# Node sums one column group ahead of the update, and a narrower last pair of tiles, in a two-layer graph network

## The chip, the core and the metric

The kernel runs on one core of a Trainium2 chip. The metric is device time in microseconds. Before the change it is 3391.78 us, the median of nine runs (3369.91 to 3401.86).

## The reference

3125 nodes with 256 features and 100,000 edges, sorted by destination, go through two layers. In each layer the features are normalised, a graph network and an attention over all nodes are added to them, and then a routed feed-forward network (mixture of experts) is added. Cut to what matters here:

```python
# layer 0, graph part: twice
agg = segment_sum(x[col], row)               # sums over neighbours
h = (x + agg / max(deg, 1)) @ W.T + b
x = silu((h - mean) * rsqrt(var + eps) * g + beta)
# layer 0, experts: 8 experts, 256 -> 1024 -> 256, the best two of each node
# layer 1, graph part: attention over the edges; then linear attention; then
# layer 1, experts: 6 experts, 256 -> 256 -> 256 -> 256, the best two of each node
h1 = relu(x @ w1[e] + b1[e]); h2 = relu(h1 @ w2[e] + b2[e]); y = h2 @ w3[e] + b3[e]
out = x + sum over the two best experts of weight * y
```

## The kernel before

**Layout.** Nodes lie in 25 tiles of 128 rows (`NB` = 25); the last tile has `LAST` = 53 real rows. `xs` holds the running features of all tiles in SBUF.

**Layer 0's graph part** (in `fast`, from line 2790). The kernel has made a dense count matrix `adj` (3125 by 3200, bf16, in DRAM) out of the edges, so that neighbour sums are matrix products. The two graph layers are one loop `for layer in range(2)`; inside it one loop goes over column groups of destination nodes: `GROUPS` is six groups of 512 columns and one of 128, and `GROUPS1`, used in the second graph layer, is five of 512, two of 256 and one of 128. They are numbered 0 to 6 and 0 to 7 below. For one column group at column `c` of width `cw`:

- *Sums.* Two PSUM tiles `agg0`, `agg1` (two slots each) collect 25 source tiles. For each source tile a bf16 piece `at` (loaded by SP, 640 KB for five source tiles, four slots) is cast to `wide` (five slots), on ScalarE (line 2834) or VectorE (line 2836) by turns, and four matmuls (line 2839) multiply it with the tile's features `px`, kept as a high and a low part. So a group has 100 matmuls. In the second graph layer the group at column 0 also makes `px` anew (`two_parts`, lines 2276 to 2278) from `yn`, which the first graph layer has written. In the first graph layer SP also issues the clearing of the experts' input table here.
- *Update.* VectorE makes `zt` from `agg`, the degrees and `xt` (lines 2844, 2845; two slots). For each 128 columns TensorE multiplies with the layer's weights (`hp`, line 2853, one slot), VectorE adds the bias and takes the statistics; then comes the normalisation and ScalarE's silu. In the first graph layer the result goes to `yn` and, transposed, back to `xt`. In the second it is added to `xs`, and `T_.tokens` routes the nodes: normalisation twice, transposes (line 375), router matmuls `lg` (line 2360), softmax and top two, positions in the experts' table (`slot`), and two scatters by POOL for each tile (line 2413) of the routed rows `x2`. `x2` has the tag `zt`, so both share its two slots; most of the small tiles of `tokens` have one slot. `tokens` of the groups depend on each other through the running count `base`.

After the last group come `T_.plan` and `T_.results`, which turn the counts into a plan, and then the experts of layer 0 (`experts`; first a transpose, line 2613).

**What sets the order there.** This part is not written out by hand: the framework's planner orders each engine's instructions when the program is built. It goes through an estimated run, and for an engine that is free it takes, among the instructions whose inputs and slots are there, the one that stands first in the program. Afterwards each engine runs its list strictly in that order. The experts of layer 0, and all of layer 1's graph part and experts, have a hand-written order instead (`manual_schedule`).

**Layer 1's experts** (`Layer1.group`). Node tiles are taken together in groups of two or three (`TOGETHER`); the last is tiles 23 and 24. For each of six experts there are two hidden layers, each of two halves `j`: two matmuls with the weights as the stationary side and the group's features as the moving side, `W = nt * 128` columns (line 1494; each f32 matmul is two records in the trace), then a relu on ScalarE (line 1497); `hp` has two slots. Then `result` multiplies the hidden features with the third weights (line 1563) and VectorE adds them, weighted, to `xs` (line 1569). Groups are spread as filler over the blocks of edges by `take`; the last group is queued when the last block's nodes are done, so it runs alone at the end of the kernel.

Of the kernel before, what the change touches and what calls it, by code (L numbers as in the profile page):

```python
# [11 lines left out]
AF = mybir.ActivationFunctionType  # L12
# [6 lines left out]
P = 128  # L19
NB = 25  # L20
NP = NB * P
LAST = N - (NB - 1) * P
GROUPS = [(c, min(512, NP - c)) for c in range(0, NP, 512)]
# [5 lines left out]
W = 8  # L29
# [942 lines left out]
GROUPS1 = GROUPS[:5] + [(2560, 256), (2816, 256), (3072, 128)]  # L972
# [379 lines left out]
class Layer1:  # L1352
# [121 lines left out]
    def group(self, t0, nt, xt):  # L1474
        nc, wk, ps, xs = self.nc, self.wk, self.ps, self.xs
        W, u = nt * P, nt / 4
        sh = [P, nt, NE1]
        k = lambda name, *d: wk.tile([P, GB] + list(d), F32, name=name, bufs=1)[:, :nt]
        bc = lambda x: x[:, :, None].to_broadcast(sh)
        ws = {}  # L1480
# [10 lines left out]
        def layer(i, e, x, o, j):  # L1491
            hp = ps.tile([P, 512], F32, name="hp", bufs=2)
            for n in range(2):
                nc.tensor.matmul(hp[:, :W], ws[i, e][:, n, j * P:(j + 1) * P], x[:, n, :W], start=(n == 0),  # L1494
                                 stop=(n == 1))
            b = self.bc1 if i == 1 else self.bc2
            nc.scalar.activation(o[:, j, :W], hp[:, :W], AF.Relu, bias=b[:, e, j:j + 1])  # L1497

        h1, h2 = {}, {}
        hid = lambda name: wk.tile([P, 2, GB * P], F32, name=name)  # L1500
# [48 lines left out]
        wgt = wk.tile([P, GB, NE1], F32, name="wgt")[:, :nt]  # L1549
# [9 lines left out]
        def result(e, i0):  # L1559
            y = two()  # L1560
            for i in range(i0, min(i0 + 2, nt)):
                for n in range(2):
                    nc.tensor.matmul(y[:, i - i0, :], h2[e][:, n, i * P:(i + 1) * P], ws[3, e][:, n, :],  # L1563
                                     start=(n == 0), stop=(n == 1))

            def add():
                for i in range(i0, min(i0 + 2, nt)):
                    t = t0 + i
                    nc.vector.scalar_tensor_tensor(xs[:, t, :], y[:, i - i0, :], wgt[:, i, e:e + 1], xs[:, t, :],  # L1569
                                                   op0=OP.mult, op1=OP.add)  # L1570
                    if e == NE1 - 1:
                        n = P if t < NB - 1 else LAST
                        self.stores.append((self.out[t * P:t * P + n, :], xs[:n, t, :]))
            self.late.append(add)

# [1111 lines left out]
def fast(ctx: ExitStack, tc: tile.TileContext, a, out, flag):  # L2687
    nc = tc.nc
# [102 lines left out]
    with tc.tile_pool(name="g", bufs=1) as g1, tc.tile_pool(name="ga", bufs=4) as ga, \  # L2791
            tc.tile_pool(name="gt", bufs=2) as gt, \
            tc.tile_pool(name="gg", bufs=2, space=PSUM) as gg, \
            tc.tile_pool(name="gp", bufs=1, space=PSUM) as gp:
        wr = load_k(nc, g1, a["L0_ffn_Wr"], "wr", nc.scalar)
        br = g1.tile([P, NE0], F32, name="br")
        nc.scalar.dma_start(br, row_bc(a["L0_ffn_br"], NE0))
        once = gt.tile([P, D], F32, name="z")[:SH, :P]
        nc.vector.tensor_reduce(once, deg[:SH].rearrange("p (k l) -> p l k", l=P), AX.X, OP.add)
        nc.vector.tensor_scalar(once, once, 1.0, None, op0=OP.max)  # L2800
        nc.vector.reciprocal(once, once)
        nc.sync.dma_start(degrees, once)
        clear = T_.clear(tc, zero)
        for t in range(0, NB, 2):
            mix.result(t, mix_p, gt, gam, xs)
        yn = nodes.tile([P, NB, D], F32, name="yn", tag="late")
        for layer in range(2):
            w = load_k(nc, g1, a[f"L0_gnn_W{layer}T"], f"gw{layer}")
            rows = {}
            for name in ("b", "g", "beta"):  # L2810
                rows[name] = g1.tile([P, D], F32, name=f"row_{name}", tag=f"row_{name}{layer}")
                nc.scalar.dma_start(rows[name], row_bc(a[f"L0_gnn_{name}{layer}"], D))
            for c, cw in (GROUPS if layer == 0 else GROUPS1):
                agg = [gg.tile([P, 512], F32, name=f"agg{g}") for g in range(2)]
                rdeg = gt.tile([P, 512], F32, name="rdeg")[:, :cw]
                nc.scalar.dma_start(rdeg, degrees.rearrange("s l -> (s l)")[None, c:c + cw].to_broadcast([P, cw]))
                for kb in range(NB // KB):
                    at = ga.tile([P, KB, 512], BF, name="at")
                    k0 = kb * KB
                    m = KB if k0 + KB < NB else KB - 1  # L2820
                    nc.sync.dma_start(at[:, :m, :cw], adj[k0 * P:(k0 + m) * P, c:c + cw].rearrange(
                        "(k p) s -> p k s", p=P))
                    if m < KB:
                        nc.sync.dma_start(at[:LAST, m, :cw], adj[full:N, c:c + cw])
                    for _ in range(4 if layer == 0 and c else 0):
                        next(clear, None)
                    for i in range(KB):
                        k = k0 + i
                        n = P if k < NB - 1 else LAST
                        if layer == 1 and c == 0:  # L2830
                            two_parts(nc, gt, px[:, 0, k, :], px[:, 1, k, :], yn[:, k, :], [P, D])
                        wide = ga.tile([P, 512], F32R, name="wide", bufs=5)
                        if (i + layer) % 2:
                            nc.scalar.copy(wide[:n, :cw], at[:n, i, :cw])  # L2834
                        else:
                            nc.vector.tensor_copy(wide[:n, :cw], at[:n, i, :cw])
                        for g in range(2):
                            for j in range(2):
                                nc.tensor.matmul(agg[g][:, :cw], px[:n, j, k, g * P:(g + 1) * P],  # L2839
                                                 wide[:n, :cw], start=(k == 0 and j == 0),  # L2840
                                                 stop=(k == NB - 1 and j == 1))
                zt = gt.tile([P, 2, 512], F32, name="zt")
                for g in range(2):
                    nc.vector.tensor_tensor(zt[:, g, :cw], agg[g][:, :cw], rdeg, OP.mult)
                    nc.vector.tensor_add(zt[:, g, :cw], zt[:, g, :cw], xt[:, g, c:c + cw])
                nt = cw // P
                h = gt.tile([P, 4, D], F32, name="h")
                st = gt.tile([P, 4, 6], F32, name="st")
                mv = gt.tile([P, 4, 2], F32, name="mv")
                for i in range(nt):  # L2850
                    hp = gp.tile([P, D], F32, name="hp")
                    for k in range(2):
                        nc.tensor.matmul(hp, zt[:, k, i * P:(i + 1) * P], w[:, k, :], start=(k == 0),
                                         stop=(k == 1))
                    nc.vector.tensor_add(h[:, i, :], hp, rows["b"])
                    nc.vector.bn_stats(st[:, i, :], h[:, i, :])
                    nc.vector.bn_aggr(mv[:, i, :], st[:, i, :])
                rs = gt.tile([P, 4], F32, name="rs")
                nc.vector.tensor_scalar(rs[:, :nt], mv[:, :nt, 1], EPS, None, op0=OP.add)
                nc.scalar.activation(rs[:, :nt], rs[:, :nt], AF.Sqrt)  # L2860
                nc.vector.reciprocal(rs[:, :nt], rs[:, :nt])
                for i in range(nt):
                    t = c // P + i
                    z = gt.tile([P, D], F32, name="z")
                    nc.vector.scalar_tensor_tensor(z, h[:, i, :], mv[:, i, 0:1], rows["g"],
                                                   op0=OP.subtract, op1=OP.mult)
                    nc.vector.scalar_tensor_tensor(z, z, rs[:, i:i + 1], rows["beta"], op0=OP.mult, op1=OP.add)
                    y = yn[:, t, :] if layer == 0 else gt.tile([P, D], F32, name="y")
                    nc.scalar.activation(y, z, AF.Silu)
                    if layer == 0:  # L2870
                        transposed(nc, C, gp, xt[:, :, t * P:(t + 1) * P], y)
                    else:
                        nc.vector.tensor_add(xs[:, t, :], xs[:, t, :], y)
                if layer == 1:
                    T_.tokens(tc, C, gt, gp, xs, c // P, nt, wr, br)
        T_.plan(nc, C, gt)
    big.close()
    late = ctx.enter_context(tc.tile_pool(name="late", bufs=1))
# [196 lines left out]
```

## Time and profile before

| | |
|---|---|
| median of nine runs | 3391.78 us (3369.91 to 3401.86) |
| profiled execution, its own time | 3373.52 us |
| its span, first to last instruction | 3371.5 us |
| mean granted TensorE clock | 0.816 |
| first graph layer's first sums | start at 371.5 us |
| second graph layer's last sums | end at 818.5 us |
| layer 0's experts, first transpose | 852.3 us |
| last pair of layer 1's experts | 3321.0 to 3364.6 us |

The profile is of one execution. "Granted clock" is the TensorE clock as a share of full speed. In a timeline row the first number is the start in us, the second the duration, then engine, line, operation, output from input, and how many instructions were merged; in brackets stands how long the engine was idle before it and what released it. A matmul's end is modelled, so consecutive matmul rows overlap a little; starts are the better measure. A row whose letters are cut, such as `x` for `x2`, names the tile without its number.

### The profile page before, as it was taken

The numbers are of one execution on the slowest core, as the hardware profiler recorded it, in microseconds if no ns is written. First come the engines' busy times: TensorE is split into PE (matmuls) and PEld (weight loads), VectorE is DVE, ScalarE is ACT, GpSimd is POOL, SyncE is SP. The second block draws the span as 40 slices with busy tenths as digits, with TensorE's granted clock in tenths as the row PEclk, the third lists the DMA queues.
The fourth block names the chain that finished last, engine by engine and source line by source line (L and its number), as shares of the span: only waits on it lengthen the run. The fifth ranks groups of instructions, "written<-read, shape, count | busy, mean of one in ns | idle before, by whom it ended". The sixth has DMA issues, their size and how long they took to land.

```text
span 3371.5 us, 35817 instructions
## 1 busy us (share of the span) xinstructions
PE 2338.2 (69%) x11721; PEld 1608.7 (48%) x11721; DVE 1690.2 (50%) x4297; ACT 902.4 (27%) x1982; POOL 1040.4 (31%) x1101
## 2 busy tenths in 40 slices
PE   4899899997777998897254536355465756545678
PEld 2555677776556887343232323243233323333446
DVE  8988766686200222632153546365546545444463
ACT  3444234553112222221121110122122212212223
POOL 1000000122463000502434444535546455454310
PEclk9999999995878999898566656687677868776789
DMA  4333596433445666545332334344435434443432
GB/s 124 74 68 68 171 299 201 133 115 101 129 130 181 199 216 209 167 162 165 88 83 81 92 84 118 107 123 124 128 103 142 125 112 134 118 135 114 117 101 82
DMA packets 432699, 440.21 MB, mean 131 GB/s; under 512 B 167736, under 2 KB 376678, under 8 KB 432372
## 3 DMA queue, kind: packets, MB, share of 16 engines
q1 hardware_dynamic: 336750, 268.60, 26.2%
q0 software_dynamic: 50128, 130.98, 13.9%
q10 hardware_dynamic: 45622, 38.21, 3.9%
q8 instruction: 96, 1.57, 0.2%
q14 instruction: 103, 0.84, 0.1%
HBM read 337.43 MB, written 100.22 MB: 130 GB/s over the span
## 4 chain that ended last, share of the span: by engine, by line
PE 20%; another core or an unknown queue 15%; issue 10%; DVE 10%; ACT 3%; DMA 1%; POOL 0%; DVEq 0%; ACTq 0%; POOLq 0%
PE hp L1494 6%; PE hp L2993 5%; PE yp L1563 3%; PE sums L1753 2%; DVE r L1747 2%; PE yp L2003 1%; ACT h L1497 1%; DVE own L1446 1%; PE yp L1892 1%; DVE ad L1448 0%; DVE ot L1425 0%; DVE tm L1683 0%; PE yp L1586 0%; PE hp L1486 0%
## 5 line engine op out<-in xcount | busy, mean ns | idle before, releaser
L1639 POOL DMA_INDIRECT r<-tab,b_at x826 | 802.7, 972 | 1002.1 <-issue 243.4
L2839 PE MATMUL agg<-wide,px 128*128 128x512 f32 (+5 forms) x1500 | 370.6, 396 | 6.2 <-DVE st_r L2341 3.4
L2839 PEld LDWEIGHTS agg<-wide,px 128*128 128x128 f32 (+1 forms) x1500 | 271.0, 206 | 61.1 <-issue 9.2
L1747 DVE TENSOR_TENSOR r<-r,fixed 128x1024 f32<-128x1024 f32 x207 | 247.1, 1209 | 83.4 <-ACT fixed L1726 78.9
L1497 ACT ACTIVATE h<-hp,bc 128x256 f32<-128x256 f32 (+1 forms) x264 | 131.4, 501 | 544.0 <-remote 294.0
L2629 PE MATMUL fhp<-fxe,fw 128*128 128x256 f32 (+1 forms) x992 | 224.5, 382 | 58.9 <-ACT fhid L2630 38.4
L1753 PE MATMUL sums<-r,oh 128*32 128x264 f32 x1652 | 180.2, 476 | 89.5 <-DVE r L1747 54.8
L1494 PE MATMUL hp<-xt,ew 128*128 128x256 f32 (+1 forms) x528 | 180.6, 473 | 71.8 <-issue 29.7
L2629 PEld LDWEIGHTS fhp<-fxe,fw 128*128 128x128 f32 x992 | 179.8, 207 | 101.9 <-ACT fhid L2630 50.7
L1563 PE MATMUL yp<-ew,h 128*128 128x256 f32 x600 | 162.1, 417 | 91.4 <-DVE xs L1817 64.2
L1494 PE MATMUL hp<-h,ew 128*128 128x256 f32 (+1 forms) x528 | 176.9, 467 | 58.6 <-issue 38.7
L2993 PE MATMUL hp<-wt,xt 128*128 128x512 f32 x400 | 186.6, 619 | 17.6 <-ACT xt L376 9.0
L2630 ACT ACTIVATE fhid<-fhp,fb 128x256 f32<-128x256 f32 (+1 forms) x248 | 109.3, 446 | 324.5 <-PE fhp L2629 193.0
L2637 PE MATMUL fyp<-fw,fhid 128*128 128x256 f32 x864 | 192.4, 380 | 0.0
L2413 POOL DMA_INDIRECT route_x<-x,slot x50 | 52.4, 1048 | 440.4 <-DVE route_at L2408 342.9
L1563 PEld LDWEIGHTS yp<-ew,h 128*128 128x128 f32 x600 | 120.0, 208 | 121.6 <-DVE xs L1817 67.0
L2637 PEld LDWEIGHTS fyp<-fw,fhid 128*128 128x128 f32 x864 | 162.5, 191 | 20.9
L1494 PEld LDWEIGHTS hp<-xt,ew 128*128 128x128 f32 x528 | 109.8, 221 | 121.3 <-issue 48.5
L1494 PEld LDWEIGHTS hp<-h,ew 128*128 128x128 f32 x528 | 106.2, 212 | 107.9 <-issue 55.1
L2959 POOL DMA_INDIRECT y<-route_y,slot x50 | 48.9, 978 | 324.5 <-DVE kv_mean L1347 294.8
L2834 ACT CAST wide<-at 128x512 fp32r<-128x512 bf16 (+5 forms) x190 | 101.6, 541 | 159.2 <-PE agg L2839 134.8
L1569 DVE SCALAR_TENSOR_TENSOR xs<-yp,wgt,xs 128x256 f32<-128x256 f32 x150 | 65.8, 474 | 148.3 <-PE yp L1563 111.3
(527 smaller groups left out, 3850.2 us busy)
## 6 DMA issues: line engine op xcount, KB each, us to landing
fw<-in_L_ffn_W SPq DMA_DIRECT2D x62, 1024.0 KB
ew<-in_L_ffn_expert_w SPq DMA_DIRECT2D x198, 256.0 KB
at<-adj SPq DMA_DIRECT2D x44, 640.0 KB
route_x<-zero SPq DMA_DIRECT2D x104, 256.0 KB
tab<-stage SPq DMA_DIRECT2D x25, 1056.0 KB
oe<-b_order ACTq DMA_DIRECT2D x117, 168.0 KB
adj<-adj_o SPq DMA_DIRECT2D x78, 250.0 KB
r<-tab,b_at POOLq DMA_INDIRECT x826
```

Source lines behind the costliest of these rows:

```text
L1494: nc.tensor.matmul(hp[:, :W], ws[i, e][:, n, j * P:(j + 1) * P], x[:, n, :W], start=(n == 0), stop=(n == 1))
L1497: nc.scalar.activation(o[:, j, :W], hp[:, :W], AF.Relu, bias=b[:, e, j:j + 1])
L1563: nc.tensor.matmul(y[:, i - i0, :], h2[e][:, n, i * P:(i + 1) * P], ws[3, e][:, n, :], start=(n == 0), stop=(n == 1))
L1639: st = self.nc.gpsimd.indirect_dma_start(out=r[:, q, c, :], out_offset=None, in_=self.table, in_offset=bass.IndirectOffsetOnAxis(ap=self.B ...
L1747: nc.vector.tensor_tensor(rv, rv, x[:, :, :, None].to_broadcast([P, n, HD, DH]), OP.mult)
L1753: mm = nc.tensor.matmul(self.sums[q * QD:(q + 1) * QD, :], ohs[j][:, q, c, :], r[:, q, c, :], start=(s0 + c == 0), stop=(s0 + c == QC - 1))
L2629: nc.tensor.matmul(hp, w1[:, k, i * P:(i + 1) * P], xe[:, k, :], start=(k == 0), stop=(k == 1))
L2630: nc.scalar.activation(hid[:, i, :], hp, AF.Gelu, bias=b1[:, 0, i:i + 1])
L2637: nc.tensor.matmul(yp, hid[:, i, t * P:(t + 1) * P], w2[:, i, :], start=(i == 0), stop=(i == K1 - 1))
L2834: nc.scalar.copy(wide[:n, :cw], at[:n, i, :cw])
L2839: nc.tensor.matmul(agg[g][:, :cw], px[:n, j, k, g * P:(g + 1) * P], wide[:n, :cw], start=(k == 0 and j == 0), stop=(k == NB - 1 and j == 1))
L2993: nc.tensor.matmul(hp.rearrange("p r d -> p (r d)"), xt[:, k, :], wt[:, k, j * 512:(j + 1) * 512], start=(k == 0), stop=(k == 1))
```

## The change

There are two edits.

In the loop over column groups, the body is split into two functions, `add_up` (loads, casts and sums) and `update` (all that follows), and the loop calls `add_up` of a group before `update` of the group before it. The last `update` of each graph layer follows the loop. Instructions, slots and sizes stay as they are; the order in the program changes.

In `group`, the last pair of tiles moves `V = 256 - 128 + 53 = 181` columns instead of 256 through the two hidden layers, and `result` of the last tile makes and adds 53 rows instead of 128. The router's matmuls keep their width.

```diff
@@ group
         W, u = nt * P, nt / 4
+        V = W if t0 + nt < NB else W - P + LAST
...
-                nc.tensor.matmul(hp[:, :W], ws[i, e][:, n, j * P:(j + 1) * P], x[:, n, :W], start=(n == 0),
+                nc.tensor.matmul(hp[:, :V], ws[i, e][:, n, j * P:(j + 1) * P], x[:, n, :V], start=(n == 0),
                                  stop=(n == 1))
...
-            nc.scalar.activation(o[:, j, :W], hp[:, :W], AF.Relu, bias=b[:, e, j:j + 1])
+            nc.scalar.activation(o[:, j, :V], hp[:, :V], AF.Relu, bias=b[:, e, j:j + 1])
...
+                rows = P if t0 + i < NB - 1 else LAST
                 for n in range(2):
-                    nc.tensor.matmul(y[:, i - i0, :], h2[e][:, n, i * P:(i + 1) * P], ws[3, e][:, n, :],
+                    nc.tensor.matmul(y[:rows, i - i0, :], h2[e][:, n, i * P:i * P + rows], ws[3, e][:, n, :],
...
-                    nc.vector.scalar_tensor_tensor(xs[:, t, :], y[:, i - i0, :], wgt[:, i, e:e + 1], xs[:, t, :],
+                    n = P if t < NB - 1 else LAST
+                    nc.vector.scalar_tensor_tensor(xs[:n, t, :], y[:n, i - i0, :], wgt[:n, i, e:e + 1], xs[:n, t, :],
@@ fast
-            for c, cw in (GROUPS if layer == 0 else GROUPS1):
+            def add_up(c, cw):
                 agg = [gg.tile([P, 512], F32, name=f"agg{g}") for g in range(2)]
...
+                return c, cw, agg, rdeg
+
+            def update(c, cw, agg, rdeg):
                 zt = gt.tile([P, 2, 512], F32, name="zt")
...
+            ahead = None
+            for c, cw in GROUPS if layer == 0 else GROUPS1:
+                sums = add_up(c, cw)
+                if ahead is not None:
+                    update(*ahead)
+                ahead = sums
+            update(*ahead)
```

More of the change, by code (lines that the diff above doesn't have):

```diff
@@ L1568, in add @@
                     t = t0 + i
-                    nc.vector.scalar_tensor_tensor(xs[:, t, :], y[:, i - i0, :], wgt[:, i, e:e + 1], xs[:, t, :],
+                    n = P if t < NB - 1 else LAST
+                    nc.vector.scalar_tensor_tensor(xs[:n, t, :], y[:n, i - i0, :], wgt[:n, i, e:e + 1], xs[:n, t, :],
                                                    op0=OP.mult, op1=OP.add)
                     if e == NE1 - 1:
-                        n = P if t < NB - 1 else LAST
                         self.stores.append((self.out[t * P:t * P + n, :], xs[:n, t, :]))
```

## Prediction

> **What bounds the kernel now.** I read the page first, then the busy time by stage over the graph layers, then the engines' timelines at the seams of that stage, then the last 50 us. S(c) is the node sums of column group c (`agg`, line 2839), U(c) its update (lines 2842 to 2875).
>
> The page's engine totals, and its 40 slices of 84 us:
>
> ```profile
> PE 2338.2 (69%) x11721; PEld 1608.7 (48%) x11721; DVE 1690.2 (50%) x4297; ACT 902.4 (27%) x1982; POOL 1040.4 (31%) x1101
> ...
> PE   4899899997777998897254536355465756545678
> DVE  8988766686200222632153546365546545444463
> ...
> PEclk9999999995878999898566656687677868776789
> ```
>
> No engine bounds the whole run. TensorE is busy in slices 5 to 9 (337 to 843 us), where the two graph layers run and the first edit works; the second works in the last slice.
>
> The graph layers by stage (stretch, its length, busy time and instructions of each engine, granted clock, DMA share):
>
> ```profile
> 371.00:562.00 191.00, 189.96 (x822) 147.65 (x823) 119.85 (x336) 68.76 (x133) 0.00 (x0) 0.99 0.79 258
> 562.00:589.00 27.00, 23.66 (x122) 21.82 (x121) 23.68 (x88) 16.96 (x44) 0.00 (x0) 0.72 0.41 118
> ...
> 709.00:741.00 32.00, 31.10 (x154) 24.61 (x153) 25.08 (x108) 17.00 (x32) 8.29 (x8) 1.00 0.33 101
> 741.00:773.00 32.00, 28.56 (x172) 27.29 (x171) 22.62 (x107) 15.44 (x35) 8.37 (x8) 0.79 0.34 98
> ...
> 797.00:819.00 22.00, 21.68 (x89) 20.06 (x89) 13.62 (x74) 10.70 (x20) 3.95 (x4) 0.50 0.07 25
> 819.00:837.00 18.00, 5.34 (x17) 3.85 (x17) 12.67 (x78) 5.35 (x9) 4.12 (x5) 0.50 0.50 148
> ```
>
> Until 741 us TensorE is full: U(c) already runs inside S(c+1), because the planner lets the ready instruction that stands first in the program go first and fills the rest with sums. After 741 us nothing is full: a chain of updates runs to 838 us, at half clock from 797.
>
> That chain, on TensorE and VectorE: first matmul of U(4), U(5), U(6), U(7), the experts' first transpose; then the routed rows `x2` and the next group's `zt`:
>
> ```profile
> 740.46 0.59 PE L2853 MATMUL hp<-gw,zt 128*128 128x256 f32 x2
> ...
> 773.02 1.02 PE L2853 MATMUL hp<-gw,zt 128*128 128x256 f32 x4
> ...
> 796.82 2.07 PE L2853 MATMUL hp<-gw,zt 128*128 128x256 f32 x4 [4.41 <-DVE zt L2845]
> ...
> 819.15 2.07 PE L2853 MATMUL hp<-gw,zt 128*128 128x256 f32 x4 [0.28 <-DVE zt L2845]
> ...
> 852.31 1.09 PE L2613 MATMUL ftp<-ident,fx 128*128 128x128 f32 x4 [14.83 <-DVE rs_rank L2526]
> ```
>
> ```profile
> 768.83 1.37 DVE L368 TENSOR_SCALAR x<-xl,mv_r,rs_r 128x256 f32<-128x256 f32 x4
> ...
> 770.22 0.41 DVE L2844 TENSOR_TENSOR zt<-agg,rdeg 128x256 f32<-128x256 f32 x1
> ...
> 788.37 0.79 DVE L368 TENSOR_SCALAR x<-xl,mv_r,rs_r 128x256 f32<-128x256 f32 x2
> ...
> 795.52 0.42 DVE L2844 TENSOR_TENSOR zt<-agg,rdeg 128x256 f32<-128x256 f32 x1 [4.69 <-DMA route_x<-x,slot]
> ```
>
> `zt` and `x2` share two slots (tag `zt`). S(6) left TensorE at 784.06, U(5)'s slot was free from 775, yet zt(6) comes only after x2(5) at 788.37 and then waits for the scatter of x2(4). So slots of a tag go out in program order: U(c+1) cannot begin before U(c) has reached `x2`.
>
> **The change, part by part.** *Same work, other order.* The first edit adds and removes no instruction. SP's list (the `at` loads and clears of `add_up`) and POOL's scatters keep their order; ACT's `rdeg` load stays in `add_up`. What moves is rank: S(c+1) now ranks above U(c), so U(c)'s matmuls get TensorE only when S(c+1) has nothing ready. Casts wait for TensorE in these stages (101 ACT and 81 DVE casts waited 134.8 and 85.5 us for `agg` matmuls), so S always has something ready: U(c) moves whole behind S(c+1) and runs beside S(c+2).
>
> *Where TensorE is full (371 to 741 us): 0.* It does the same matmuls in 189.96 of 191 us. S(6) of the first layer, 128 columns, has beside it another update of four tiles; its stall (3.8 us idle at 561 to 574) stays. Bounds: -4 if it goes, +3 if U(5) and U(6), now both beside the second layer's first sums, delay the parts of tiles 20 to 24.
>
> *The end of layer 1: +15.* At S(4)'s end U(3)'s TensorE work is not yet done: 16 `hp` records of 0.22, 8 transposes of 0.19, 16 `lg` of 0.13 = 7.1 us. S(4) therefore ends at 738.2 - 7.1 = 731.1, and U(3) begins there instead of at 708.70: 22.4 later. From there, with the rows of before:
> - hp(3) to x2(3): 26.3 beside 512-column sums (708.70 to 734.95), 28.4 beside 256 (740.46 to 768.83); S(5) has 256. x2 to the next hp: 4.2. hp(4) = 731.1 + 28.4 + 4.2 = 763.7, or 761.6 with 26.3. Middle 762.6 (was 740.46).
> - hp(4) to hp(6): 56.4 as before (740.46 to 796.82), since zt(6) still waits for the scatter of U(4): slots at +43.4, eight scatters in 10.0, landing 1.7, zt 1.3. hp(6) = 819.0.
> - hp(6) to hp(7) was 22.3, of which some 3.3 was S(7)'s late end at 818.4 (x2(6) was there at 813.60). Now S(7) is long done: 19.0. hp(7) = 838.0.
> - hp(7) to the experts' first transpose: 33.2, unchanged. Shift 838.0 - 819.15 = 18.9.
> Lighter load beside U(5) and U(6), whose casts are gone, should give back some 4 (13 casts of 0.2 to 0.3 us and a hp that no longer queues behind sums). I take +15; bounds +8 (the 3.6 and 1.4 us of VectorE stalls inside U(4) and the 4.7 of the scatter shrink too) and +19. The experts' rows start behind the last scatter and their weights are there by then (issued at 832), so the shift passes on whole.
>
> *181 columns: -5.* The last pair has 48 `hp` matmuls in 96 records and 24 relus. In the last 28 us, at clock 0.96, this is TensorE's pace:
>
> ```profile
> 3343.65 1.03 PE L1494 MATMUL hp<-xt,ew 128*128 128x256 f32 x4
> 3344.52 1.03 PE L1494 MATMUL hp<-h,ew 128*128 128x256 f32 x4
> ...
> 3344.78 0.47 ACT L1497 ACTIVATE h<-hp,bc 128x256 f32<-128x256 f32 x1 [2.45 <-PE hp L1494]
> ```
>
> A record takes 0.218 us start to start, at 181 columns 0.154: 56 records save 3.6. The relu falls from 0.47 to some 0.41 (casts of 512, 256, 128 columns: 0.62, 0.41, 0.30), and the third and fourth layer call of an expert now wait about 0.18 for it in two `hp` slots: four experts give back 0.7. Twelve records at half clock (0.43 each) save 1.5, the 28 before 3332, in a chain of relu and routing, some 0.7. Sum 5.1. `result` streams the same 256 columns with a narrower stationary side, and the DVE add is as long on 53 partitions: 0. A row speaks for less: a 128-column weight load lasts 0.188, and if matmuls could not follow each other faster the 56 records would save 1.7 and the sum be 2.8. A row against it lies nearer: 29 sums of 128 columns, each with its own load, took 3.54 us, 0.122 each (567.98).
>
> The Trainium skill (TensorE: Matmul & The Clock Gate, LDWEIGHTS) counts a load as columns over 1.2 GHz, 107 ns for 128. By that rule the load is no floor at 181 columns and the saving stays 5.1; by the 0.188 row it would be 2.8.
>
> The rule that speaks against this change is the same page's, on the clock gate: after an idle window of about 3.4 us TensorE runs at half clock. The rows here agree (0.50 from 797). Doing the sums early leaves a longer end without dense matmuls; but U(6) and U(7) run at half clock already, so by the rule the sum stays at +10.
>
> **Sum.** 0 + 15 - 5 = +10 us. The profiled execution took 3373.5 (span 3371.5), 18.3 under the median of the nine runs; it would take 3383.5, and the median 3391.8 becomes 3402. This is just at 0.3% (10.2 us), about what a measurement of this kernel can tell from no change.
>
> **Rivals.**
> - *The order hardly changes* (the planner finds gaps in S(c+1) and puts U(c) in them): 0 - 5 = -5, 3387. For it: TensorE did idle 0.8 us at 699 and 731. Against: the casts' waits above. 0.12.
> - *Sums early, updates free: faster.* If `zt` got any free slot, U(c+1) could start while U(c) is still short of `x2`, and with S(5) to S(7) out of the way U(5) to U(7) would overlap: S(7)'s 3.3 us, the 4.7 us scatter wait and the 3.8 us of layer 0 go, -11.8, with the last pair -17: 3375. It decides as soon as zt(4) runs ahead of x2(3). For it: VectorE works only 63.5 of the 96 us from 741 to 837. Against: zt(6)'s place behind x2(5). 0.20.
> - *Tail lag as costed:* 0.65; its own range 3394 to 3411. Dearer still, with stalls of tiles 20 to 24 in layer 1: 0.03.
>
> **Numbers.** The first case lies around the 0.3% line: 0.43 slower, 0.22 same. Rivals: 0.09 same and 0.03 faster; 0.17 faster and 0.03 same; 0.03 slower. Together faster 0.20, same 0.34, slower 0.46. The range from 3378 (most of the fast rival left out) to 3414 (upper bound +19 - 3, and the spread of medians) leaves out 2 in 10.
>
> **What would show it.** Right: `hp` of the first layer's group 0 follows all of S(1), TensorE stays full to about 730, S(7) ends before U(5)'s or U(6)'s `hp`, the last scatter comes at about 853 instead of 840.5, and the last pair's records are 181 wide at 0.15 to 0.16. Wrong: `hp` rows inside S(c+1); zt(c+1) ahead of x2(c); the experts' first transpose at 852 or before; records at 0.19.

## The result and the profile after

The changed kernel takes 3412.2 us (median of 20 runs, 3395.0 to 3428.8) against 3383.0 for the kernel before (62 runs). The ratio is 1.0088, with a 95% interval of 1.0071 to 1.0105: some 30 us slower. The prediction had the side and, for the lag, the mechanism; its size was +10. That 3412.2 lies inside its range of 3378 to 3414 is luck in part: the range is set on 3391.8 for the kernel before, which took 8.7 us less in these 62 runs. As a difference the range is -14 to +22 us, and the measured +29 lies outside it.

The profiled execution took 3421.99 us, its span 3420.2. The page's engine totals, and TensorE's busy share and clock in its 40 slices (now 85.5 us each):

```profile
PE 2350.6 (69%) x11721; PEld 1608.0 (47%) x11721; DVE 1693.3 (50%) x4297; ACT 898.2 (26%) x1980; POOL 1038.7 (30%) x1101
...
PE   4899899987666999798263535465555656554678
...
PEclk9999998995777999899575657677677778776779
```

The work is the same (PE has as many records, its busy time differs by 0.5%). In slices 9 to 13, from 684 us on, TensorE is 8, 7, 6, 6 and 6 tenths busy at a clock of 9, 5, 7, 7 and 7 tenths; before it was 9, 7, 7, 7 and 7 at 9, 5, 8, 7 and 8. The end of the graph layers (slices 9 and 10) has become emptier. Slices 11 to 13 hold layer 0's experts, whose length differs between executions of either kernel (below).

The graph layers by stage; the columns are as in the table of before:

```profile
371.00:584.00 213.00, 206.62 (x912) 165.52 (x912) 133.00 (x393) 78.04 (x160) 0.00 (x0) 0.95 0.76 247
...
736.00:767.00 31.00, 23.85 (x154) 21.98 (x155) 23.67 (x103) 14.66 (x32) 8.23 (x8) 0.88 0.33 97
767.00:798.00 31.00, 24.49 (x141) 21.31 (x139) 22.29 (x103) 12.62 (x30) 8.20 (x8) 0.78 0.22 63
798.00:831.00 33.00, 29.38 (x124) 27.49 (x124) 19.44 (x110) 12.85 (x27) 8.66 (x9) 0.50 0.10 35
831.00:865.00 34.00, 12.59 (x37) 8.33 (x36) 21.93 (x113) 12.78 (x21) 7.23 (x9) 0.50 0.26 77
```

TensorE is full until 736 (busy for 148 of the 152 us from 584), as foretold. Then follow four stages of 31 to 34 us instead of four of 32, 24, 22 and 18, and those at a clock of 0.50 all through make up 67 us instead of 40.

The chain on TensorE: `hp` of U(3) to U(7), two rows of sums between them, and the experts' first transpose:

```profile
735.86 1.13 PE L2858 MATMUL hp<-gw,zt 128*128 128x256 f32 x4
...
767.44 1.05 PE L2858 MATMUL hp<-gw,zt 128*128 128x256 f32 x2
...
797.04 1.33 PE L2841 MATMUL agg<-wide,px 128*128 128x128 f32 x5 [0.92 <-DVE zt L2849]
798.17 2.02 PE L2858 MATMUL hp<-gw,zt 128*128 128x256 f32 x4
...
828.49 2.99 PE L2841 MATMUL agg<-wide,px 128*128 128x128 f32 x12
831.41 2.07 PE L2858 MATMUL hp<-gw,zt 128*128 128x256 f32 x4
...
847.59 2.07 PE L2858 MATMUL hp<-gw,zt 128*128 128x256 f32 x4 [1.15 <-DVE zt L2850]
...
881.34 1.09 PE L2615 MATMUL ftp<-ident,fx 128*128 128x128 f32 x4 [14.91 <-DVE rs_rank L2528]
```

Before, `hp` of U(3) stood here:

```profile
708.70 0.59 PE L2853 MATMUL hp<-gw,zt 128*128 128x256 f32 x2
```

`hp` of U(3) stands at 735.86 instead of 708.70, the transpose at 881.34 instead of 852.31: 29.0 us, as much as the median lost (29.2). S(7) begins only at 797.04, when `zt` of U(5) has read the sums of group 5: `agg` has two slots, so S(7) cannot run earlier, whatever its rank. Its last 12 matmuls come at 828.49, and U(6) stands behind them. On VectorE, `zt` of U(6) was ready at 824.6:

```profile
822.88 0.42 DVE L2849 TENSOR_TENSOR zt<-agg,rdeg 128x256 f32<-128x256 f32 x1 [4.93 <-DMA route_x<-x,slot]
...
824.18 0.41 DVE L2850 TENSOR_TENSOR zt<-zt,xt 128x256 f32<-128x256 f32 x1
```

So U(6) first waits for the scatter, as it did before, and then 6.8 us more. Some 4 of them are sums of S(7), a group that is not yet wanted. The rest is the counts of U(5) (`lg` from `own`), which stand between these sums in TensorE's list and make it idle for 2.19 us:

```profile
827.62 0.61 PE L2400 MATMUL lg<-own,after 128*128 128x16 f32 x2 [2.19 <-DVE own L2396]
```

The last pair, one expert to the next (the third layer `yp`, then a hidden layer of the next expert):

```profile
3395.86 0.78 PE L1495 MATMUL hp<-h,ew 128*128 128x181 f32 x4
3396.47 2.02 PE L1565 MATMUL yp<-ew,h 128*128 128x256 f32 x8
3398.43 0.88 PE L1495 MATMUL hp<-xt,ew 128*128 128x181 f32 x4
```

The last four records of an expert take 0.61 us (0.153 each); an expert takes 4.73 us (the next `yp` is at 3401.20) against 5.21 before (`yp` at 3347.14 and 3352.35).

### The profile page after: what moved, and what is told of

It is laid out like the page before. It is cut to its first block, busy times and chain, and to the rows that moved or that the text cites. A ratio compares the mean times of both kernels' runs of the same rounds, so it can differ in the third digit from the quotient of the medians.

```text
span 3420.2 us, 35824 instructions
## 1 busy us (share of the span) xinstructions
PE 2350.6 (69%) x11721; PEld 1608.0 (47%) x11721; DVE 1693.3 (50%) x4297; ACT 898.2 (26%) x1980; POOL 1038.7 (30%) x1101
## 4 chain that ended last, share of the span: by engine, by line
PE 19%; another core or an unknown queue 15%; issue 10%; DVE 10%; ACT 3%; DMA 1%; POOL 0%; ACTq 0%; DVEq 0%; SPq 0%
PE hp L1495 6%; PE hp L3006 4%; PE yp L1565 3%; PE sums L1755 2%; DVE r L1749 2%; ACT h L1498 1%; DVE own L1446 1%; DVE ot L1425 1%; PE hp L1487 1%; PE yp L1894 0%; DVE tm L1685 0%; DVE ad L1448 0%; PE yp L1588 0%; PE yp L2005 0%
## 5 line engine op out<-in xcount | busy, mean ns | idle before, releaser
L1498 ACT ACTIVATE h<-hp,bc 128x256 f32<-128x256 f32 (+2 forms) x264 | 129.8, 495 | 525.7 <-remote 268.9
L1495 PE MATMUL hp<-xt,ew 128*128 128x256 f32 (+2 forms) x528 | 186.2, 486 | 79.3 <-issue 30.5
L1495 PE MATMUL hp<-h,ew 128*128 128x256 f32 (+2 forms) x528 | 175.0, 463 | 63.1 <-ACT h L1498 51.0
L1565 PE MATMUL yp<-ew,h 128*128 128x256 f32 (+1 forms) x600 | 159.7, 411 | 69.7 <-DVE xs L1819 34.3
L1565 PEld LDWEIGHTS yp<-ew,h 128*128 128x128 f32 (+1 forms) x600 | 115.2, 201 | 100.9 <-DVE xs L1819 36.7
L1572 DVE SCALAR_TENSOR_TENSOR xs<-yp,wgt,xs 128x256 f32<-128x256 f32 (+1 forms) x150 | 65.8, 474 | 160.9 <-PE yp L1565 119.2
```

Source lines behind the costliest of these rows:

```text
L1495: nc.tensor.matmul(hp[:, :V], ws[i, e][:, n, j * P:(j + 1) * P], x[:, n, :V], start=(n == 0), stop=(n == 1))
L1498: nc.scalar.activation(o[:, j, :V], hp[:, :V], AF.Relu, bias=b[:, e, j:j + 1])
L1565: nc.tensor.matmul(y[:rows, i - i0, :], h2[e][:, n, i * P:i * P + rows], ws[3, e][:, n, :], start=(n == 0), stop=(n == 1))
```

## The experiments

They ran on three chips. The kernel before took 2665.0 us on that of the first four kernels, 3428.8 on that of the next four, and on the third 3430.0 beside three kernels and 3394.6 beside the last. Every ratio is against runs of before taken on the same chip with the kernel. The times in the graph layers agree between the chips to some 5 us. "Transpose" is the experts' first transpose; all columns but the second are starts in the timeline of the profiled execution.

| kernel | ratio, 95% interval | hp of U(3) | transpose |
|---|---|---|---|
| before | 1 | 708.70 | 852.31 |
| changed | 1.0088 (1.0071 to 1.0105) | 735.86 | 881.34 |
| cols_only | 0.9997 (0.9988 to 1.0007) | 708.89 | 848.56 |
| order_only | 1.0109 (1.0094 to 1.0125) | 733.33 | 877.55 |
| first_layer | 1.0016 (1.0007 to 1.0025) | 710.11 | 853.74 |
| second_layer | 1.0115 (1.0100 to 1.0131) | 732.32 | 878.40 |
| hold_early | 1.0068 (1.0041 to 1.0095) | 733.08 | 878.06 |
| hold_tail | 1.0038 (1.0010 to 1.0067) | 709.74 | 864.53 |
| after_own1 | 1.0076 (1.0048 to 1.0105) | 719.11 | 879.87 |
| cols_own1 | 0.9978 (0.9955 to 1.0001) | 709.46 | 850.57 |
| wide_333 | 0.9980 (0.9961 to 0.9999) | 708.03 | 846.30 |
| cols_32 | 0.9986 (0.9963 to 1.0009) | 710.04 | 836.33 |
| after_333 | 1.0114 (1.0074 to 1.0154) | 736.91 | 872.06 |
| wide_32 | 0.9939 (0.9919 to 0.9958) | 706.65 | 834.19 |

**The two edits apart: cols_only and order_only.** The first keeps the second edit and has a loop that holds no update back; the second has the changed loop and no second edit (`V` is `W`, and `rows` is `P`). The loop of the first serves in other experiments too, which differ in the condition after `hold` alone:

```diff
-            ahead = None
+            waiting = []
             for c, cw in GROUPS if layer == 0 else GROUPS1:
-                sums = add_up(c, cw)
-                if ahead is not None:
-                    update(*ahead)
-                ahead = sums
-            update(*ahead)
+                waiting.append(add_up(c, cw))
+                hold = False                               # cols_only
+                while len(waiting) > (1 if hold else 0):
+                    update(*waiting.pop(0))
+            while waiting:
+                update(*waiting.pop(0))
```

> The second edit alone: 181 columns in the last pair, the loop over column groups as before. Theory (the two edits are independent, and the relu's hand-over gives part of the saving back): from the last transpose of features (before 3319.82) to the end 48.3 us instead of 51.7, as in the changed kernel, so -3.4 us in all and a ratio of 0.999. The prediction's own sum was -5.1. Rival (a weight load of 0.188 us paces the records): records of hp 0.19 apart and -2.8 or less. The graph layers stay: experts' first transpose at 852 +/- 2.

> The first edit alone: node sums one group ahead, 256 columns in the last pair. Theory (all of the loss is the first edit): experts' first transpose at 881, 29 us later than before, and a ratio of 1.0098, 0.1% above the changed kernel's 1.0088. Rival (part of the loss lies behind the graph layers, in the experts of layer 0, which took 496.0 us from first transpose to last matmul in the changed kernel's profile and 482.6 before): the 881 again, the experts at 496 again, and a ratio of up to 1.013.

The order alone makes 1.0109, and its transpose is 29.0 us behind that of cols_only on the same chip, where the whole kernel loses 27.7 (2692.67 - 2665.02): all of the loss is the first edit and lies ahead of the transpose. The rival fell: layer 0's experts take 406.2 us here and 405.6 in cols_only. The 13 us between the two first profiles (495.9 and 482.6) is a spread of the slower chips: with the order of before it is 477.9 in cols_32 and 501.5 in wide_32. The 181 columns alone bring 0.5 us, with 0 in the interval; an expert takes 4.73 us again (`yp` at 2634.24 and 2638.97). From the last transpose of features to the end it takes 48.5 us, near the expected 48.3; but the three runs with 256 columns on its chip (order_only, first_layer, second_layer) take 49.4 to 50.2 there, not the 51.7 of the first profile, so the saving is some 1 to 2 us instead of 3.4. The pace of a record (0.153) is not the 0.19 of the rival. wide_333 below says what an expert loses again.

**Which layer: first_layer and second_layer** (256 columns in both).

```diff
+                hold = layer == 0                          # first_layer
+                hold = layer == 1                          # second_layer
```

> Node sums ahead in the first graph layer only, 256 columns in the last pair. Theory (the lag costs at the end of the second layer alone): no change of time, ratio 0.999 to 1.001. In the first layer the sums of the last group end 4.4 us sooner than before, counted from the first sums, as in the changed kernel; the second layer's first group gives that back, since it then has U(5) and U(6) beside it (30.6 us instead of 27.0); hp of group 3 in the second layer at 709 to 712, experts' first transpose at 852 to 856. Rival (the lag is taken along from the first layer): hp of group 3 at 731 or later and a ratio of 1.006 or more.

> Node sums ahead in the second graph layer only, 256 columns in the last pair. Theory (the lag of one group is taken on in the second layer and shows at its end): hp of group 3 at 730 to 733 instead of 708.70, experts' first transpose at 876 to 879, +24 to +27 us, ratio 1.007 to 1.008. Rival (the loss comes from the seam of the layers or the first layer): transpose at 852 to 860, ratio under 1.003.

The second layer alone costs all of it, 29.6 us (2694.59 - 2665.02), and `hp` of U(3) is at 732.32 as expected. The first layer alone was expected to cost nothing and costs 4.3 us. Its last sums end 4.2 us sooner, counted from the first sums (211.1 us against 215.3 in cols_only), and S(0) of the second layer then takes 30.8 us instead of 26.9: that exchange is as expected. Of the 5.2 us at the transpose, 1.2 are there at U(3) and 3.6 arise between `hp` of U(4) and of U(5) (33.5 us against 29.9 in cols_only). There the granted clock differs: from 760 to 770 us it is 0.50 in first_layer and in before, which with the old order needs 32.6, and 0.67, then 1.00 in cols_only. So these 3.6 us don't show a price of the edit; whether the 4.3 us of the medians are one stays open.

**Where in the second layer: hold_early and hold_tail.** Only some updates are held behind the next sums: U(0) and U(1), or U(5) and U(6).

```diff
+                hold = layer == 1 and c < 1024             # hold_early
+                hold = layer == 1 and c >= 2560            # hold_tail
```

> In the second layer only U(0) and U(1) are held behind the next group's sums; from group 2 on the order is the old one (S0 S1 U0 S2 U1 U2 S3 U3 and so on); 256 columns in the last pair. Theory (a chain of updates takes 30 to 32 us a group, as much as TensorE needs for a group, so a lag taken on early is never made good): hp of group 3 at 728 to 733 (before 708.70), experts' first transpose at 872 to 878, loss of 20 to 26 us, ratio 1.0075 to 1.010. Rival (the loss is made at the end, by sums of the last groups in front of U(4) to U(7)): hp of group 3 back at 709 to 712, transpose at 850 to 856, ratio under 1.002.

> In the second layer only U(5) and U(6) are held behind the sums of S(6) and S(7); everything before is in the old order; 256 columns in the last pair. Theory (the lag counts where TensorE is full; after 741 us it has room, and U(5) waits for x2 of U(4) anyway): hp of group 4 at 740 as before, of group 5 at 769 to 774, experts' first transpose at 847 to 856, time within 4 us of before, ratio 0.9985 to 1.0015. Rival (the sums of the narrow groups in front of the updates are what costs): transpose at 862 or later, ratio above 1.004.

hold_early puts the transpose at 878.06, though from group 2 on its order is the old one; the whole kernel loses 20 us (1.0068), a little under the expected ratio. `hp` of U(2) and U(3) are at 701.22 and 733.08; before they were at 676.87 and 708.70. Both are 24 us late, and 31.9 apart instead of 31.8. Here a chain of updates needs 31 to 32 us a group, and so does TensorE, so a lag of one group's sums is not made good. Its price is paid once: from the first sums to the transpose hold_early takes 507.7 us, the changed kernel, which holds every update back, 507.9, and before 480.9.

hold_tail went against the theory: U(4) is on time (741.62) and yet the transpose is 12 us late. TensorE and VectorE at the place:

```profile
775.89 0.42 DVE L2848 TENSOR_TENSOR zt<-zt,xt 128x256 f32<-128x256 f32 x1
```

```profile
781.43 2.70 PE L2839 MATMUL agg<-wide,px 128*128 128x256 f32 x19
784.06 1.13 PE L2856 MATMUL hp<-gw,zt 128*128 128x256 f32 x4
```

`zt` of U(5) is ready at 776.3, its first matmul comes at 784.06, behind the end of S(6): 7.8 us in which TensorE runs almost only sums that no update waits for yet. And S(6) ends no sooner than before (784.1 against 782.6; the 784.06 of the prediction is the end of a merged row that holds the first sums of S(7) too): its rank does not help it, between 762 and 771 us it gets four matmuls every two or three us. U(6) then waits behind S(7) in the same way, for 10.0 us, since its `zt` is ready at 804.7:

```profile
814.69 2.07 PE L2856 MATMUL hp<-gw,zt 128*128 128x256 f32 x4
```

U(7), for which S(7) is then out of the way, follows after 16.1 us instead of 22.3. So sums in front of an update cost here too, without the lag of the earlier groups.

**The shared slots: after_own1 and cols_own1.** `zt` and `x2` get one slot each; the first is the changed kernel so altered, the second has the order of before and 181 columns.

```diff
-                zt = gt.tile([P, 2, 512], F32, name="zt")
+                zt = gt.tile([P, 2, 512], F32, name="zt", bufs=1)
...
-        x2 = wk.tile([P, 2, 512], F32, name="x2", tag="zt").rearrange("p a (b d) -> p (a b) d", d=D)
+        x2 = wk.tile([P, 2, 512], F32, name="x2", bufs=1).rearrange("p a (b d) -> p (a b) d", d=D)
```

> The changed kernel with one slot of its own for zt and one for x2, instead of two that they share. Theory (updates follow each other at 31.5 us because the slots are handed out in the order of the program, x2 of a group before zt of the next): zt(c+1) now runs ahead of x2(c), hp of group 4 comes 20 us after hp of group 3 or less instead of 31.6, experts' first transpose at 855 to 868 instead of 877 to 881, ratio 1.001 to 1.006. Rival (VectorE's work and the one-slot tiles of the routing hold the updates apart, slots or not): hp to hp 30 us or more, transpose at 875 or later, ratio 1.009 to 1.011.

> The kernel before with 181 columns in the last pair and one slot of its own for zt and one for x2. Theory (zt of group 6 waits for the scatter of x2 of group 4 only because they share slots): hp of group 6 comes 10 us sooner than the 793 to 797 of before, hp of group 7 and the experts' first transpose 5 to 9 us sooner (840 to 844), ratio 0.9965 to 0.998. Rival (the wait moves on to the routing of group 5 or to S(7), which then stands behind U(6)): transpose at 848 to 850, ratio 0.9995 to 1.0005.

The slots do set the order, as the prediction said: freed, `zt` of U(1) runs ahead of `x2` of U(0), and `hp` of U(1) follows that of U(0) by 15.9 us (638.73 and 654.66). VectorE in after_own1:

```profile
645.18 0.68 DVE L2849 TENSOR_TENSOR zt<-agg,rdeg 128x512 f32<-128x512 f32 x1
...
664.53 1.37 DVE L368 TENSOR_SCALAR x<-xl,mv_r,rs_r 128x256 f32<-128x256 f32 x4
```

But it brings nothing: the transpose is at 879.87. The counts of the groups (`own`, line 2400) come 32.7 us apart (675.0, 707.7, 740.6, 773.2), and U(3), whose `hp` is now at 719, reaches its `own` 54 us later, where before it took 38. The second rival of the prediction, "sums early, updates free", is gone: its condition was met and the time stayed. What holds the routing then (VectorE's order, its one-slot tiles, the scatter that `x2` waits for) was not taken apart. In cols_own1, `hp` of U(6) goes 8 to 11 us sooner (785.67; 793.33 in cols_only, 796.82 before), and the gain stops at S(7), which, as before, ends right in front of U(7), at 819.45, for `hp` at 819.73; the transpose is where it was, and the ratio of 0.9978 has 1 just inside its interval.

**Fewer groups at the end: wide_333, cols_32, after_333.** If the end is a chain of updates with a fixed part each, fewer of them should help. wide_333 also gives the third layer its 128-wide stationary side back.

```diff
-GROUPS1 = GROUPS[:5] + [(2560, 256), (2816, 256), (3072, 128)]
+GROUPS1 = GROUPS[:4] + [(2048, 384), (2432, 384), (2816, 384)]   # wide_333, after_333
+GROUPS1 = GROUPS[:5] + [(2560, 384), (2944, 256)]                # cols_32, wide_32
...
+                if V < W: nc.gpsimd.memset(h2[e][:, :, V:W], 0.0)  # wide_333, wide_32
...
-                    nc.tensor.matmul(y[:rows, i - i0, :], h2[e][:, n, i * P:i * P + rows], ws[3, e][:, n, :],
+                    nc.tensor.matmul(y[:, i - i0, :], h2[e][:, n, i * P:(i + 1) * P], ws[3, e][:, n, :],
```

> The order of before; two other things changed. (1) The second layer's last four groups (512, 256, 256, 128 columns) become three of 384. Theory (the end is a chain of updates with a fixed part in each): an interval between the 31.6 us of a 512 group and the 23.8 of a 256 group, some 27.5, so hp of groups 5 and 6 at 768 and 796, the last group's own 33 us later, experts' first transpose at 840 to 847 instead of 852, ratio 0.996 to 0.998. Rival (the sums of 384 columns come late, or the longer last update gives it back): transpose at 850 or later, ratio 0.999 to 1.001. (2) 181 columns in the hidden layers of the last pair, but the third layer's stationary side 128 wide for both tiles again (the unused part of h2 is set to zero on GpSimd). Theory (a switch between a 128-wide and a 53-wide stationary side costs 0.09 us, twice an expert): an expert takes 4.55 us instead of 4.73 (181 and 53) and 5.21 (256 and 128). Rival (the relu's hand-over alone makes the difference): 4.73 again.

> The order of before with 181 columns in the last pair, and the second layer's last three groups (256, 256, 128 columns) made into two (384, 256). Theory (a fixed part for each update): groups 5 and 6 at 773 and 796 to 802, last own 30 us later, experts' first transpose at 840 to 847, ratio 0.996 to 0.998. Rival: S(6), twice as wide as the old last group, comes late and the transpose is at 850 or later, ratio 0.999 to 1.001.

> The changed kernel with three last groups of 384 columns in the second layer instead of 512, 256, 256 and 128. Theory (the lag of one group is worth about one group's sums whatever the last groups are): hp of group 3 at 730 to 736, experts' first transpose 18 to 28 us later than with the order of before and the same groups (so 860 to 872), ratio 1.003 to 1.008. Rival (the loss comes from narrow groups, whose sums hold TensorE at half clock): at most 8 us later than with the order of before, ratio under 1.0.

With the order of before, two last groups put the transpose at 836.33, three of 384 at 846.30, eight groups at 848.6 to 852.3. after_333 is 25.8 us behind wide_333: the lag costs nearly the same without any group of 256 or 128 columns, and the rival fell. Its ratio of 1.0114 is above what was expected; the part behind the transpose is not explained. cols_32 is 12 to 16 us sooner at the transpose and shows 0.9986 with 1 inside its interval; the runs of before beside it alone lie between 3411.8 and 3448.5.

With the wide third layer an expert of the last pair takes 4.42 us, better than the 4.55 expected. What the 53 rows cost is seen in the weight loads (PEld), first of before, then of the changed kernel:

```profile
3346.92 1.70 PEld L1563 LDWEIGHTS yp<-ew,h 128*128 128x128 f32 x8
```

```profile
3396.32 0.78 PEld L1565 LDWEIGHTS yp<-ew,h 128*128 128x128 f32 x4
3397.43 0.60 PEld L1565 LDWEIGHTS yp<-ew,h 128*53 128x53 f32 x4 [0.33 <-issue]
3398.43 0.60 PEld L1495 LDWEIGHTS hp<-xt,ew 128*128 128x128 f32 x4 [0.39 <-issue]
```

Before, the loads of the eight `yp` follow each other without a gap and begin 0.22 us ahead of the first of their matmuls (3347.14), under the matmul before it. Where the stationary side goes from 128 columns to 53, and back, the loads have a gap of 0.33 and 0.39 us. The eight `yp` records of an expert take 1.96 us (3396.47 to 3398.43) instead of 1.72 (3347.14 to 3348.86); the rest of the 0.31 us between 4.73 and 4.42 lies in the `hp` records behind them.

**Both gains together: wide_32.**

> A version meant to beat both kernels: the order of before, the second layer's last three groups made into two (384, 256), 181 columns in the hidden layers of the last pair, and the third layer 128 wide for both tiles (the unused part of h2 set to zero on GpSimd). Theory (the two gains are in different stages and add): experts' first transpose at 834 to 842 as with the two groups before, an expert of the last pair at 4.42 us as with the wide third layer, together 13 to 20 us less than before, ratio 0.994 to 0.996 where a run of before takes 3430, 0.993 to 0.995 where it takes 2665. Rival (time gained ahead of layer 0's experts is lost there or in the edge blocks, as the ratio of 0.9986 with its transpose 16 us sooner might say): ratio 0.998 to 1.000.

It takes 3373.5 us against 3394.6: 0.9939 (0.9919 to 0.9958), 21 us less than before, the best of all, and a little more than the two gains were expected to make. Where all of it comes from is not shown: cols_32 has the same groups and lacks the wide third layer alone, and had 7 us less than before (13 less to 3 more); of the 14 us between the two, 0.31 us for each of six experts makes 2. U(5), U(6) and the transpose, on TensorE, and an expert of the last pair:

```profile
769.81 1.17 PE L2861 MATMUL hp<-gw,zt 128*128 128x256 f32 x4 [0.55 <-DVE zt L2853]
...
794.25 2.07 PE L2861 MATMUL hp<-gw,zt 128*128 128x256 f32 x4 [2.41 <-DVE zt L2853]
...
834.19 1.08 PE L2618 MATMUL ftp<-ident,fx 128*128 128x128 f32 x4 [15.74 <-DMA fb<-in_L_ffn_b1c]
...
3360.96 1.89 PE L1566 MATMUL yp<-ew,h 128*128 128x256 f32 x8
...
3365.38 1.89 PE L1566 MATMUL yp<-ew,h 128*128 128x256 f32 x8
```

The update that had followed U(6) is gone, with its 22 us from `hp` to `hp`; U(5), one tile larger, does not make the last `hp` later (794.25, that of U(6) before 796.82; both 425 us after the first sums).

## Why the prediction was right, and where its size was wrong

The terms of its sum beside the two first profiles:

| term of the sum | predicted | measured |
|---|---|---|
| first sums start (ahead of the change) | 0 | +1.9 (371.46, 373.40) |
| from there to the end of S(0) of the second layer | 0 (-4 to +3) | +0.7 (242.2, 242.9) |
| from there to hp of U(3) | +22.4 | +24.5 (95.1, 119.6) |
| hp(3) to hp(4) | -0.3 | -0.2 (31.8, 31.6) |
| hp(4) to hp(6) | 0 | +7.6 (56.4, 64.0) |
| hp(6) to hp(7) | -3.3 | -6.2 (22.3, 16.2) |
| hp(7) to the transpose | 0 | +0.6 (33.2, 33.8) |
| lighter load beside U(5) and U(6) | -4 | none |
| sum | +15 | +29.0 |
| 181 columns | -5.1 | -0.5 in cols_only |

**Right.** The planner does what was read out of the casts' waits: U(c) goes whole behind S(c+1) (`hp` of the first layer's group 0 at 443.96, where S(1) ends). The slots of `zt` go out in the order of the program (`x2` of U(3) at 762.59, `zt` of U(4) at 763.98). The full stage costs nothing, though not as its bounds say. The first layer's last sums end 4.5 us sooner, but the stall that the bound of -4 names stays (3.9 us idle from 556 to 570): they end sooner because the TensorE work of U(5) now comes behind them. It comes back as 1.5 us in front of S(0) and +3.6 in it, which has U(5) and U(6) beside it. The lag of one group's sums, the term that carries the sum, is 24.5 instead of 22.4, and the shift passes on whole. (The slices of TensorE that the prediction calls 5 to 9 are 5 to 10, 337 to 843 us.)

**The term that was mis-sized** is the end of layer 1, +15. The step that failed is "Now S(7) is long done", and with it "S(7) ends before U(5)'s or U(6)'s `hp`" (the last scatter comes at 869.5, not at 853). Two slots of `agg` keep S(7) from starting before `zt` of U(5); the prediction had itself put U(c) beside S(c+2), and did not carry that to S(7). So hp(4) to hp(6) isn't "as before": U(6) waits 6.8 us behind sums that now rank above it and the counts between them. Of the 7.6 us, 2.9 come back up to U(7), for which S(7) is then out of the way; 4.7 are left. hold_early, with the old order at the end, has no such wait and takes 57.5 and 19.9 us there, near the 56.4 and 19.0 of the sum. But its U(4) comes 33.9 us after U(3) instead of 31.6, and it is no sooner at the transpose, so no run shows that the time would fall if the wait alone went. The 4 us that lighter load should give back did not come: S(6) from 764.7 and S(7) from 797.0 to 831.5, with their casts, still lie beside U(4), U(5) and the start of U(6). The rest of the 14 us are small: +2.1 in the lag, +0.7 in the full stage, +0.6 behind U(7), and +1.9 that stood there before the change acts and is the spread of a run (the first sums start between 368.7 and 373.4 in these profiles, whatever the order).

**181 columns.** For the expert that repeats, the sum said -1.02 in sixteen records and +0.18 in the relu's hand-over, -0.84. The changed kernel has -0.48 (5.21 to 4.73). The step that failed is "`result` streams the same 256 columns with a narrower stationary side: 0", which cost 0.31: without that side, wide_32 has -0.79. The hand-over is near what was said: the sixteen records take 2.69 us there (3362.69 to 3365.38), where 0.154 each would be 2.47, so it costs some 0.22. In front of the repeating part the 1.5 and 0.7 of the sum don't show: from the last transpose of features to the first `yp` cols_only takes 20.1 us, the three runs with 256 columns on its chip 19.8 to 20.7. A record's own pace was right (0.153 for 0.154), and the weight load of 0.188 us is no floor: the row of the 128-column sums held. (With that floor the prediction's own terms give 3.2, not 2.8.)

The load records last 0.19 us for 128 columns and 0.13 for 53, while records with a load each follow each other at 0.153 and 0.122. The Trainium skill (TensorE: Matmul & The Clock Gate, LDWEIGHTS) counts a load by its columns. The 107 ns for 128, an estimate by its formula, lies under both paces, so as a floor it isn't contradicted here; but the records of the loads are longer, and they don't go in proportion to the columns.

**The clock.** The prediction kept its sum by saying that U(6) and U(7) run at half clock already; so they do, at 0.50 before and after. But the clock is half from some 786 us on in both profiles, and the lag moves U(5) behind that: four records of its `hp` take 2.02 us instead of 1.02. The prediction has no term for this, and no run shows its price alone. By the Trainium skill (TensorE: Matmul & The Clock Gate, the HAM clock gate) an idle stretch of some 3.4 us halves the clock, and the prediction found its rows to agree. They do in part: in the changed kernel the clock falls to 0.50 behind an idle stretch of 3.49 us (in front of 785.99); in before it falls between 783 and 787 although TensorE was busy from 773 to 783 and was idle for 0.81 us at most up to 787.

## What to carry to other kernels

Giving producers a higher rank than consumers moves every consumer behind one whole producer step; where the consumers' chain needs as long a step as the producer's engine, this lag is paid in full at the end, as here, and a stage that was full before has nothing to win. Before work is called "long done", count the slots of its output and ask which consumer must release one. At the end of such a chain, cut the number of its links (two last groups instead of three: 12 to 16 us at the transpose) rather than reorder them, and when only the moving side is cut, leave the stationary side's width alone.

## What the runs showed of the hardware

A change of the stationary side's width between neighbouring matmuls, 128 to 53 columns and back, cost 0.24 us in the eight `yp` records of an expert and 0.31 with the records behind them (4.73 against 4.42 us): at each change the loads have a gap of 0.33 or 0.39 us, which at one width is not there. The Trainium skill (TensorEngine Tiling (Array Packing), Tiling Modes) says that changing the tiling mode drains TensorE. The gaps of 0.33 and 0.39 us in the loads agree with that, if 53 columns are another mode than 128, which no run here shows.

The same program takes 2665 us on one chip and 3383 to 3430 on the others. Up to the experts' first transpose they agree (848.6 and 852.3 us, in cols_only and in before, which differ in the last pair alone). Behind it the experts of layer 0 take 405.6 and 482.6 us, and the edge blocks from first to last `sums` 1085.7 and 1626.3. In before, ScalarE's relu `h` (line 1497) waits 294 us in 28 waits for something that the profile of this core doesn't name (it calls it `remote`); among the longest waits of cols_only there is none of that kind. What it is was not tested.
